# Side steps, softplus steps and sums: a new order on TensorE in a four-layer selective-scan kernel

## The chip, the cores and the metric

The kernel runs on one core of a Trainium2 chip. The metric is device time in microseconds (us) of one execution; the time of a kernel is the median of several executions.

## The reference, cut to what matters

Four layers are applied one after another to `x` of shape (8, 48, 48, 96): `x = x + layer(groupnorm(x))`. Each layer is a two-dimensional selective scan with 192 inner channels, 16 states per channel and four scan directions (rows, columns, and both backwards), over L = 2304 positions:

```python
xz = x @ in_proj_w.T;  xc, z = split(xz)            # 192 + 192 channels
u  = silu(depthwise_conv3x3(xc) + conv_b)
xs = 4 orders of u                                  # rows, columns, both reversed
dts, B, C = split(x_proj(xs))                       # rank r, 16 states, 16 states
delta = softplus(dt_proj(dts) + dt_bias)
h = exp(delta * A) * h + (delta * u) * B            # a scan over the 2304 positions
y = sum over the 16 states of h * C, plus u * D     # the four directions are added
out = (layernorm(y) * silu(z)) @ out_proj_w.T
```

Layers 0 to 2 are computed this way. Layer 3 writes the scan with cumulative sums and a division by the decay, and needs only the ends of the sequence when the decay fades; the kernel computes those ends and a test at the end decides whether the whole is needed.

## The kernel before, in words

Eight images are worked on in four pairs, so there are 3 x 4 = 12 (layer, pair) turns in the long part of the program. A turn has 12 groups (three tiles of 128 channels: image 0's first 128, image 1's first 128, and the last 64 of both; times two orders; times two directions). A group has three **chunks** of 768 positions, and a chunk has 16 **units**, n = 0 to 15, each for one 128 x 768 tile of states. That is 432 chunks and 6912 units. In this long part the instructions of each engine run in the order in which the program writes them (`keep_order`).

One unit k with its n is one pass of the loop in `run`. In the order of the text it issues:

- `collected()`: if a chunk's sum has been finished, ScalarE copies it out of PSUM (`collect`, line 887).
- `get_ready(k + 1)`: SyncE issues the loads of C (tile `cb`, nine buffers, four units ahead) and, for n in (2, 5, 7, 10, 13, 15), of B (tile `bb`, three buffers, five units ahead). For the other ten n, TensorE makes B of the next unit in PSUM (tile `b`, two buffers, line 678, `spread_rows`); for the six, GpSimd weighs `bb` with `du` (line 757, three units ahead) and ScalarE's exponential of the next unit goes to that PSUM buffer (line 780). So B(n) below is the product for unit n, issued in unit n - 1, and there is none for n in (2, 5, 7, 10, 13, 15).
- `c.scan(n)`: VectorE multiplies (line 810, only for the ten n with a B product) and scans (line 814); GpSimd multiplies `cb` by the result (line 823).
- The **sum** of unit k - 2: `add_up(n)` adds two `cb` tiles into the PSUM tile `acc` with `twin` (line 870, four recorded matmuls). It adds in pairs: `add_up` of an odd n is the first that needs `cb` of that n, from GpSimd; `add_up` of an even n brings nothing new and is the last use of both tiles of the pair before it, so it frees two `cb` buffers. Sum(16) is the second half of the pair (14, 15). `begin_sum` (line 855) starts a chunk's `acc` ahead of sum(1), and has to wait for the copy of the chunk before, since `acc` has one buffer.
- `beside()`: one step of `prepare` for the next chunk, and one side step. A side step is one step of the generators for the next turn's input (`prologue`: convolution, projections) or for the turn that is finished (`epilogue`: layer norm, gate, output product). They yield some 510 steps a turn.

`prepare` goes one step a unit, in two halves of 384 positions: the small product of `dts` (line 614) in units 15 and 6; ScalarE's functions (lines 622 to 628) in 0, 1 and in 7, 8; **softplus's sums** (line 634, two steps of eight recorded matmuls each, on tiles `du` and `dl`) in 2, 3 and in 9, 10; ScalarE's copies of `dl` (line 589) and VectorE's product with u in 4 and in 11, 12; the copies of `du` (line 589) in 5 and 13.

Before the change the sum comes ahead of `beside()` in a unit, with three exceptions. Sum(16) is issued two units after its chunk's sum(14), in unit 2 of the next chunk (`rest_of_sum`). In that unit (`ends`) no side step is taken. And in the unit after it, n = 3, where `collected()` had something to do (`busy`), `beside()` comes ahead of `begin_sum` and sum(1).

Of the kernel before, what the change touches and what calls it, by code (L numbers as in the profile page):

```python
# [53 lines left out]
NS = 16  # L54
# [49 lines left out]
def ss2d_layers_kernel(ctx: ExitStack, tc: tile.TileContext, x_in, consts, weights, out):  # L104
# [470 lines left out]
    def load_dt(c):  # L575
        r = layers[c.l].rank
        c.dts = sm1.tile([64, SCAN], F32, name="dts", tag="dts")
        for b in c.batches:
            q0 = 32 * b if c.t == 2 else 0
            nc.sync.dma_start(  # L580
                c.dts[q0 : q0 + r, : c.m],
                state[c.l, c.p]["xd"][c.ph, b, c.d * r : (c.d + 1) * r, c.c0 : c.c0 + c.m],
            )
# [101 lines left out]
    def store_some(n):  # L685
        for _ in range(min(n, len(late_stores))):
            o, z, at = late_stores.pop(0)
            nc.sync.dma_start(o[:, at], z[:, at])

    def collected():  # L690
        some = bool(late_sums)
        while late_sums:
            late_sums.pop(0)()
        return some

    def catch_up():
        while late_act:
            nc.scalar.copy(*late_act.pop(0))
# [450 lines left out]
    def drain(g):  # L1149
        for _ in g:  # L1150
            pass

    def step(g):
        next(g, None)
# [7 lines left out]
    def side_step(*sides):  # L1162

        for s in sorted(sides, key=lambda s: (not s.held, s.made / s.total)):
            got = next(s.g, s)
            s.held = got is True
            if got is not s and got is not GATED:
                s.made += 1
                return True
        return False  # L1170
# [3 lines left out]
    def mark():  # L1174
        marks.append(len(tc._region_blocks()[0].instructions))
# [12 lines left out]
    LAG = 2  # L1188
    LOADS, DECAYS = 3, 2

    def run(pairs, short):


        def units():
            for l, p in pairs:
                for gi, (t, ph, d) in enumerate(groups):
                    if l in short:
                        c = Edge(l, p, t, ph, d)
                        for i in range(NS // QUAD):
                            yield (l, p, gi * (NS // QUAD) + i), c, i  # L1200
                        continue
                    group = {}
                    for i in range(len(SCANS)):
                        c = Chunk(l, p, t, ph, d, i, group, c if d == 1 and i == 0 else None)
                        for n in range(NS):
                            yield (l, p, (gi * len(SCANS) + i) * NS + n), c, n

        def begin(l, p, first=False):
            if l not in layers:
                layers[l] = Layer(l)  # L1210
            return prologue(l, p, l in short, first)

        todo = list(units())

        def rest_of_sum(k):
            before = todo[k - 1][1] if k > 0 else None
            if isinstance(before, Chunk) and (k == len(todo) or todo[k][1] is not before):
                before.add_up(NS)

        def get_ready(k):  # L1220

            def early(ahead, what):
                for i in range(0 if k == 0 else k + ahead, min(k + ahead + 1, len(todo))):
                    getattr(todo[i][1], what)(todo[i][2])

            early(LOADS + 1, "load_b")
            early(LOADS, "load")
            if k == 0:
                todo[0][1].decay(todo[0][2])
            if k < len(todo):  # L1230
                (l, p, _), c, n = todo[k]
                if n == 0 and c.first and l not in short:
                    c.group["carry"] = capool.tile([P, NS], F32, name="carry", tag="carry")
                c.spread(n)
            early(DECAYS, "weigh")
            for i in range(k + DECAYS if k else 1, min(k + DECAYS + 1, len(todo))):
                todo[i][1].decay(todo[i][2])

        rest = begin(*pairs[0], first=True)
        while next(rest) is not READY:  # L1240
            pass
        rest = Side(rest)
        chunks = list(dict.fromkeys(c for _, c, _ in todo))
        drain(prepare(chunks[0]))
        behind = ahead = Side()
        coming = iter(())
        done = None
        mark()
        get_ready(0)
        for k, ((l, p, unit), c, n) in enumerate(todo):  # L1250
            at = pairs.index((l, p))
            following = pairs[at + 1] if at + 1 < len(pairs) else None
            if l in short and unit == 0:
                mark()
            per = NS // QUAD if l in short else NS
            all_units = len(groups) * (per if l in short else len(SCANS) * per)
            place["tiles"] = 3 * unit // all_units
            store_some(1)
            if done:
                behind, done = Side(epilogue(*done), 199), None  # L1260
            if unit == LAG and following:
                ahead = Side(begin(*following), 311)
            if k == 0:
                coming_to = 1
                coming = prepare(chunks[coming_to])
            if n == max(0, per - 1 - DECAYS):
                while coming_to < len(chunks) and not chunks[coming_to].ready:
                    next(coming)
            if n == 10 and coming_to + 1 < len(chunks):
                z = chunks[coming_to + 1]  # L1270
                if (z.l, z.p) == (l, p):
                    load_dt(z)
            busy = collected()
            get_ready(k + 1)
            catch_up()
            c.scan(n)
            if n == per - 1:
                drain(coming)
                if unit + 1 + per == all_units:
                    drain(behind.g)  # L1280
                    drain(ahead.g)
                coming_to = chunks.index(c) + 2
                coming = prepare(chunks[coming_to]) if coming_to < len(chunks) else iter(())


            def beside():
                step(coming)

                for _ in range(10 if l in short else 0 if ends else 1):
                    side_step(rest) or side_step(behind, ahead)  # L1290

            ends = l not in short and k > LAG and todo[k - LAG][2] == 0
            if busy and l not in short:
                beside()
            if k >= LAG:
                (bl, bp, _), b, bn = todo[k - LAG]
                rest_of_sum(k - LAG)
                if bl in short:
                    collected()
                b.add_up(bn)  # L1300
                if k > LAG and todo[k - LAG - 1][0][:2] != (bl, bp):
                    done = todo[k - LAG - 1][0][:2]
            if not (busy and l not in short):
                beside()
        for i in range(len(todo) - LAG, len(todo)):
            collected()
            rest_of_sum(i)
            todo[i][1].add_up(todo[i][2])
            catch_up()
        collected()  # L1310
        rest_of_sum(len(todo))
        collected()
        drain(epilogue(*pairs[-1]))

    last = NLAYER - 1
    run([(l, p) for l in range(NLAYER) for p in range(NPAIR)], (last,))

    keep_order(*marks[:2])
# [8 lines left out]
    with tc.If(nc.values_load(again, min_val=0, max_val=1) > 0):  # L1327
        run([(last, p) for p in range(NPAIR)], ())
# [95 lines left out]
```

## Time and profile before

| | |
|---|---|
| median of 5 runs | 20209.35 us (20192.55 to 20231.08) |
| profiled execution: own time / its span | 20228.16 us / 20226.3 us |
| busy over the span: PE, DVE, ACT, POOL | 83%, 87%, 80%, 88% |
| long part (layers 0 to 2), 178 to 18320 us | 18142 us: DVE busy 16758.65, POOL 17055.39, PE 15109.06, ACT 14719.72 us |
| layer 3 and the end, 18320 to 20226 us | 1906 us: PE busy 1569.34, ACT 1432.13 us |
| granted TensorE clock, long part | 0.91 |
| DMA share, long part | 0.86, 224 GB/s |

PE is TensorE, DVE VectorE, ACT ScalarE, POOL GpSimd, SP SyncE, which issues all loads. "Idle before" is the time for which an engine did nothing just before an instruction, and the name behind the arrow is what ended that time. In the long part a chunk takes 42.0 us (18142 / 432) and a unit 2.62 us.

### The profile page before, as it was taken

The numbers are of one execution on the slowest core, as the hardware profiler recorded it, in microseconds if no ns is written. First come the engines' busy times: TensorE is split into PE (matmuls) and PEld (weight loads), VectorE is DVE, ScalarE is ACT, GpSimd is POOL, SyncE is SP. The second block draws the span as 40 slices with busy tenths as digits, with TensorE's granted clock in tenths as the row PEclk, the third lists the DMA queues.
The fourth block names the chain that finished last, engine by engine and source line by source line (L and its number), as shares of the span: only waits on it lengthen the run. The fifth ranks groups of instructions, "written<-read, shape, count | busy, mean of one in ns | idle before, by whom it ended". The sixth has DMA issues, their size and how long they took to land.

```text
span 20226.3 us, 314848 instructions
## 1 busy us (share of the span) xinstructions
PE 16810.3 (83%) x92962; PEld 7791.0 (39%) x92962; DVE 17668.9 (87%) x14161; ACT 16225.3 (80%) x30014; POOL 17769.3 (88%) x10121
## 2 busy tenths in 40 slices
PE   7887887887888888888888888888888887888886
PEld 3333433333333333333333333333333333335555
DVE  6999998998999999999999999999999989996553
ACT  6777887887887887887887887877877877877786
POOL 6999999999999999999999999999999999995442
PEclk9998998998998999999998999998998988988997
DMA  5888888888888898888888888888888888884221
GB/s 157 229 226 223 227 224 217 226 223 218 224 228 224 223 232 223 225 228 224 223 229 222 222 226 224 222 224 220 223 224 222 224 221 222 219 219 115 80 74 50
DMA packets 2021150, 4200.80 MB, mean 208 GB/s; under 512 B 375920, under 2 KB 789360, under 8 KB 2017904
## 3 DMA queue, kind: packets, MB, share of 16 engines
q1 hardware_dynamic: 2019440, 4180.55, 79.5%
q8 instruction: 762, 12.48, 0.3%
q14 instruction: 948, 7.77, 0.2%
HBM read 4026.64 MB, written 152.27 MB: 207 GB/s over the span
## 4 chain that ended last, share of the span: by engine, by line
PE 21%; ACT 17%; DVE 14%; DMA 11%; issue 9%; POOL 3%; SPq 2%; DVEq 0%; POOLq 0%; ACTq 0%
DVE da L814 7%; PE acc L870 5%; PE ps L634 4%; DMA bb<-xd 4%; DMA cb<-xd 4%; DVE b L810 4%; ACT b L780 3%; ACT dl L589 3%; PE ps L314 3%; PE b L678 2%; ACT du L589 2%; POOL cb L823 2%; DVE bb L814 2%; ACT da L780 2%; SPq L740 1%
## 5 line engine op out<-in xcount | busy, mean ns | idle before, releaser
L823 POOL TENSOR_TENSOR cb<-cb,da 128x768 f32<-128x768 f32 x4320 | 7835.0, 1818 | 752.3 <-issue 258.2
L870 PE MATMUL acc<-cb,twin 128*64 128x384 f32 x27648 | 7206.5, 539 | 750.1 <-POOL cb L823 736.7
L814 DVE TENSOR_TENSOR_SCAN da<-da,carry,b 128x768 f32<-128x768 f32 x2880 | 5223.0, 1814 | 176.0 <-DVE b L810 1.4
L757 POOL TENSOR_TENSOR bb<-bb,du 128x768 f32<-128x768 f32 x2592 | 4717.1, 1820 | 236.5 <-DMA bb<-xd 131.1
L823 POOL TENSOR_TENSOR cb<-cb,bb 128x768 f32<-128x768 f32 x2592 | 4706.5, 1816 | 104.1 <-DVE bb L814 46.5
L810 DVE TENSOR_TENSOR b<-du,b 128x768 f32<-128x768 f32 x4320 | 4084.8, 946 | 707.3 <-PE b L678 603.7
L678 PE MATMUL b<-brow,pick 96*64 96x512 bf16 (+2 forms) x18816 | 2866.0, 354 | 1870.4 <-DVE da L814 1469.9
L780 ACT ACTIVATE da<-dl,a 128x768 f32<-128x768 f32 x4320 | 4011.6, 930 | 217.8 <-POOL cb L823 187.3
L870 PEld LDWEIGHTS acc<-cb,twin 128*64 128x64 f32 x27648 | 2450.1, 150 | 3042.8 <-POOL cb L823 1372.6
L814 DVE TENSOR_TENSOR_SCAN bb<-b,carry,bb 128x768 f32<-128x768 f32 x1728 | 3109.2, 1799 | 107.1 <-ACT b L780 37.0
L780 ACT ACTIVATE b<-dl,a 128x768 f32<-128x768 f32 x2592 | 2335.3, 901 | 608.5 <-DVE da L814 582.1
L678 PEld LDWEIGHTS <-pick 96*64 96x64 bf16 x18816 | 1084.1, 115 | 4140.0 <-DVE da L814 2681.6
L814 DVE TENSOR_TENSOR_SCAN da<-da,b 128x768 f32<-128x768 f32 x1440 | 2524.8, 1753 | 87.4 <-DVE b L810 0.5
L314 PE MATMUL ps<-pad,diag 128*64 128x480 f32 (+1 forms) x8640 | 2339.7, 568 | 32.9 <-ACT du L589 22.7
L589 ACT COPY dl<-ps 64x384 f32<-64x384 f32 x3456 | 1632.4, 472 | 708.7 <-PE ps L634 669.6
L634 PE MATMUL ps<-du,cst 128*64 128x384 f32 (+1 forms) x7296 | 1735.4, 512 | 75.4 <-ACT du L628 62.5
L589 ACT COPY du<-ps 64x384 f32<-64x384 f32 x3456 | 1633.4, 473 | 199.3 <-DVE ps L645 109.3
L814 DVE TENSOR_TENSOR_SCAN bb<-b,bb 128x768 f32<-128x768 f32 x864 | 1502.0, 1738 | 144.4 <-ACT b L780 76.5
L634 PE MATMUL ps<-dl,cst 128*64 128x384 f32 (+1 forms) x7296 | 1487.8, 483 | 0.0
L614 PE MATMUL ps<-dts,w 6*128 6x384 f32 (+5 forms) x2432 | 955.6, 602 | 205.8 <-DMA dts<-xd 106.6
L314 PEld LDWEIGHTS ps<-pad,diag 128*64 128x64 f32 x8640 | 753.3, 139 | 882.1 <-issue 727.6
L622 ACT ACTIVATE du<-ps,w 128x384 f32<-128x384 f32 (+1 forms) x912 | 519.9, 570 | 709.4 <-PE ps L614 694.6
(144 smaller groups left out, 19165.4 us busy)
## 6 DMA issues: line engine op xcount, KB each, us to landing
cb<-xd SPq DMA_DIRECT2D x13952, 192.0 KB
bb<-xd SPq DMA_DIRECT2D x5184, 192.0 KB
brow<-xb SPq DMA_DIRECT2D x864, 72.0 KB
ey<-yd SPq DMA_DIRECT2D x256, 216.0 KB
cb<-xd SPq DMA_DIRECT2D x128, 384.0 KB
yd<-y SPq DMA_DIRECT2D x216, 192.0 KB
ex<-xs SPq DMA_DIRECT2D x256, 108.0 KB
xb<-parts SPq DMA_DIRECT2D x96, 216.0 KB
```

What stands on the lines that cost most here:

```text
L314: nc.tensor.matmul(ps[half, :m], ly.diag[:, int(t == 2), j, half], pad[:, r0 + dy : r0 + dy + nr, dx : dx + W], start=(j == 0), stop=(j == 8),
L589: nc.scalar.copy(z[64 * h : 64 * h + 64, g, at], v[64 * g : 64 * g + 64])
L614: nc.tensor.matmul(o[:, :m], ly.dtw[q0 : q0 + r, k, chans], dts[q0 : q0 + r, at], start=True, stop=True,)
L622: nc.scalar.activation(e, v, AF.Abs, bias=bias)
L634: nc.tensor.matmul(v[half], ident[:, half], z1, start=(i == 0), stop=(i == 3))
L678: nc.tensor.matmul(o[64 * h : 64 * h + 64], pick[:, b, n : n + 1].to_broadcast([2 * NR, 64]), rows, start=True, stop=True,)
L757: nc.gpsimd.tensor_mul(b, b, self.du[n % 2])
L780: nc.scalar.activation(da, self.dl[n % 2], AF.Exp, scale=layers[self.l].a2[:, int(self.t == 2), n % 2, k, i : i + 1],)
L810: nc.vector.tensor_mul(b, self.du[n % 2], b)
L814: nc.vector.tensor_tensor_scan(way(h), way(da), way(b), start, ALU.mult, ALU.add)
L823: nc.gpsimd.tensor_mul(c, c, h)
L870: nc.tensor.matmul(self.acc[64 * g : 64 * g + 64, a, : self.m // 2], twin, c[:, a, :], start=False, stop=(pair + 2 == NS and not self.turns),)
```

## The change

Three things move; nothing is added to or taken from the arithmetic.

- In every unit the step of `prepare` and the side step are issued between B and the sum, where the sum came first.
- Sum(16) is issued together with sum(15), in unit 1 of the next chunk and not in unit 2; so `collected()` copies `acc` out in unit 2 and not in unit 3.
- Side steps by unit: none in n = 3, 9 and 10 (`full`); in n = 12 and 14 (`free`, where there is no B product to issue) a second one behind the sum; one in every other n, 2 included. Before it was none in n = 2 and one in every other. Both make 15 a chunk.

In layer 3 the step of `prepare` is issued ahead of the sum, and the ten side steps stay behind it; that part is put in order by the scheduler, not by `keep_order`.

```diff
+    full, free = (3, 9, 10), (12, 14)
+
     def run(pairs, short):
...
-        def rest_of_sum(k):
-            before = todo[k - 1][1] if k > 0 else None
-            if isinstance(before, Chunk) and (k == len(todo) or todo[k][1] is not before):
-                before.add_up(NS)
+        def sum_of(c, n):
+            c.add_up(n)
+            if isinstance(c, Chunk) and n == NS - 1:
+                c.add_up(NS)
...
-            busy = collected()
+            collected()
             get_ready(k + 1)
             catch_up()
             c.scan(n)
...
-            def beside():
-                step(coming)
-
-                for _ in range(10 if l in short else 0 if ends else 1):
+            def beside(some):
+                for _ in range(some):
                     side_step(rest) or side_step(behind, ahead)
 
-            ends = l not in short and k > LAG and todo[k - LAG][2] == 0
-            if busy and l not in short:
-                beside()
+            step(coming)
+            if l not in short:
+                beside(n not in full)
             if k >= LAG:
                 (bl, bp, _), b, bn = todo[k - LAG]
-                rest_of_sum(k - LAG)
                 if bl in short:
                     collected()
-                b.add_up(bn)
+                sum_of(b, bn)
                 if k > LAG and todo[k - LAG - 1][0][:2] != (bl, bp):
                     done = todo[k - LAG - 1][0][:2]
-            if not (busy and l not in short):
-                beside()
+            beside(10 if l in short else n in free)
         for i in range(len(todo) - LAG, len(todo)):
             collected()
-            rest_of_sum(i)
-            todo[i][1].add_up(todo[i][2])
+            sum_of(todo[i][1], todo[i][2])
             catch_up()
-        collected()
-        rest_of_sum(len(todo))
         collected()
         drain(epilogue(*pairs[-1]))
```

## The prediction

> **What bounds the kernel now.** I read the page's busy times first, then the waits, then the order of time on PE, and last SyncE's own waits. The stretches' busy times split the span:
>
> ```profile
> 178.00:18320.00 18142.00, 15109.06 (x81627) 6637.35 (x81629) 16758.65 (x12601) 14719.72 (x27223) 17055.39 (x9680) 0.91 0.86 224
> 18320.00:20226.00 1906.00, 1569.34 (x10806) 1101.85 (x10802) 899.75 (x1538) 1432.13 (x2664) 708.04 (x424) 0.89 0.26 71
> ```
>
> The columns are PE, PE's weight loads, DVE, ACT, POOL, then clock, DMA share and GB/s. In the long part POOL is busy for 94% and DVE for 92%, so POOL can win at most 18142 - 17055 = 1087 us and DVE 1383. A chunk costs POOL 22 products of 1.82 us, 40.0 us of its 42.0. No engine alone is the bound; time is lost where one hands over late. The waits name the places:
>
> ```profile
> PEld acc L870 <- POOL cb L823: 1372.6, 1045, 4.8
> ACT dl L589 <- PE ps L634: 669.6, 414, 4.8
> DVE b L810 <- PE b L678: 603.7, 646, 10.5
> POOL cb L823 <- issue: 272.8, 311, 7.7
> DVE b L810 <- PE acc L870: 93.5, 67, 4.8
> ```
>
> (us in total, times, longest.) DVE loses 603.7 + 93.5 = 697 us to a B that comes late. I gave each idle stretch to the unit whose scan ends next (6912 scans, 16 a chunk). Of the 697 us, 260 lie at n = 1, 196 at n = 11, 55 at n = 12, 67 at n = 6, 44 at n = 3, 38 at n = 0. POOL's 1088 us: 249 at n = 2, 163 at n = 7, 139 at n = 15, 110 at n = 0, 83 at n = 10, 59 at n = 12. PE in order of time shows how n = 11 and 12 come about:
>
> ```profile
> 9002.08 0.19 PEld L870 LDWEIGHTS acc<-cb,twin 128*64 128x64 f32 x2 [2.46 <-POOL cb L823]
> 9002.53 1.70 PE L634 MATMUL ps<-du,cst 128*64 128x384 f32 x7
> 9004.16 1.05 PE L472 MATMUL ps<-u,w 128*96 128x480 f32 x2
> 9005.14 0.52 PE L678 MATMUL b<-brow,pick 96*64 96x512 bf16 x4
> 9005.70 0.96 DVE L810 TENSOR_TENSOR b<-du,b 128x768 f32<-128x768 f32 x1 [0.51 <-PE b L678]
> 9006.14 1.46 PE L634 MATMUL ps<-dl,cst 128*64 128x384 f32 x8
> 9007.64 1.94 ACT L589 COPY dl<-ps 64x384 f32<-64x384 f32 x4 [1.55 <-PE ps L634]
> ```
>
> In unit 9 PE stands 2.46 us at sum(7) until GpSimd has made cb(7); only then come softplus's first sums, a side step (a projection) and B(11), for which DVE waits. None of what stood behind the sum needed cb(7). Over 432 chunks sum(7) starts 1.96 us before cb(7) is done and lasts 3.02 us where 0.81 is usual.
>
> **The change part by part.**
>
> *Softplus's sums ahead of sum(7) (units 9, 10).* Eight matmuls take 1.3 us start to start (9002.53, less the overlap, to 9004.16 with the eighth in front). They fit into the wait of 1.96. Side step 9, 0.67 us of PE in the mean (0 to 1.25), leaves, and side step 10, 0.64, too. Between cb(7) and B(11) stand only the tail of sum(7), 1.06 us, in place of 1.06 + 1.3 + 0.67 = 3.03. B(11) starts 1.08 us after its buffer is free (scan 9), so it can come 1.08 sooner and no more; its end is late by up to 1.5 us in nine of ten chunks (against scan 10), and the idle mean is 196 / 432 = 0.45. B(12) starts 2.05 us after its buffer is free and gains more. I take 200 of the 196 + 55 = 251 us off DVE, and most of ACT's 669.6 us wait for the same sums. DVE's time counts only where POOL then waits less: POOL's idle in n = 10 to 15 is 83 + 37 + 59 + 9 + 21 + 139 = 348 us, part of it for loads. Bounds: 60 (POOL already lags by a product at n = 10 and 11 and hides it) and 300. A measure from the trace: in 88 chunks where units 9 and 10 happen to have no side work on PE, scans 8 to 15 take 20.50 us, against 20.80 in the rest; 0.30 x 432 = 130 us for that half of the edit alone. I take 150 us of gain.
>
> *All other odd sums behind the steps.* Sums 5, 11 and 13 wait less (they last 1.11, 0.94, 1.15 us against 0.81); with sum(13) in a late B(1) at most 0.3 us a chunk. What is behind them on PE is the same B as before. I take 30 us, bounds 0 and 110.
>
> *Sum(16) a unit sooner, side step 3 to unit 2.* B(3) now stands behind sum(16): 0.74 us at full clock, 1.3 at half. PE waits 327 us in 320 chunks for scan 1 before B(3), 0.76 us a chunk, and B(3)'s end is a median 1.07 ahead of need; sum(15) lasts 1.85 us, so side step 1 slips into its wait. Cover is there in most; where PE is cold it is missing. Cost 25 us, bounds 0 and 120. B(4) trades sum(16) for side step 2, B(6) loses and gains one step: nothing. The copy of `acc` on ACT goes from unit 3 to unit 2; it waits for PE for 264 us now and would for sum(16) again, but ACT's own queue there holds a carry and, two units on, an exponential: nothing. Buffers of cb(14), cb(15) come free a unit sooner, before load cb(7).
>
> *Second side steps in 12 and 14.* They take 2 x 0.66 us of PE where PE waits for DVE's buffers, 464 us at n = 13 and 607 at n = 15 (3.0 us a chunk with the smaller waits). Hidden as long as that lasts. But B(12) now comes about 1.5 us sooner, so PE's wait there is about 3.0 + 1.5 - 1.3 - 0.6 (DVE sooner) = 2.6 us: little less than before.
>
> That matters for the clock. The chunk's start runs on PE at half rate:
>
> ```profile
> 9018.29 0.85 PE L678 MATMUL b<-brow,pick 96*64 96x512 bf16 x4 [3.43 <-DMA brow<-xb]
> 9020.35 1.54 PE L614 MATMUL ps<-dts,w 16*64 16x384 f32 x4
> 9024.56 0.96 DVE L810 TENSOR_TENSOR b<-du,b 128x768 f32<-128x768 f32 x1 [2.58 <-PE b L678]
> ```
>
> B took 0.85 us here and 0.52 above; the granted clock was 0.57 from 9016 to 9032 and 1.00 from 9000 to 9009. In all chunks, half rate holds 1.89 of the 2.89 us of unit 0 and 1.88 of the 3.42 of unit 1, and 7.7 us of a chunk. From the waits I take no gain at n = 1 beyond the 30 us above: 2.6 against 3.0 us. The Trainium skill ("TensorE: Matmul & The Clock Gate", section "Part 1: The HAM clock gate (the "warmup" mystery)") says that the clock is halved only after an idle window of about 3.4 us, and is whole again after as long a busy one; by that rule a step in the middle of the wait of units 14 and 15 would keep the clock up in most chunks, and the sum would be some 150 us lower. The trace goes cold in most chunks with waits that mean 1.4 to 1.9 us each, which speaks against so sharp a rule, so it is a rival and not in the sum.
>
> *Sums that free buffers for loads come later.* SyncE issues in order:
>
> ```profile
> SPq L740 <- PE acc L870: 1859.4, 1736, 6.5
> POOL bb L757 <- DMA bb<-xd: 131.1, 108, 4.4
> ```
>
> Most of the 1859 us belong to cb(5) on sum(14) (620 us, 293 times), cb(9) on sum(2) (303), cb(15) on sum(8) (293), cb(13) on sum(6) (198). Queued behind cb(15) on SP: both `brow` loads, cb(0) and bb(2). bb(2) lands a median 1.08 us before POOL takes it, within 0.2 in a quarter of the chunks; POOL idles 140 us there. The others land 2.4 to 3.6 us ahead. Sum(8) ends 4.21 us after cb(7) now; after the change, scan 9 (1.95 after cb(7)) + B 0.52 + softplus 1.3 + sum 0.81 = 4.6, later by 0.4. In the tight quarter to half that is 45 to 85 us; sum(14) and sum(6) behind one side step more (0.7 us) eat margin that is there. I take 50, bounds -40 (DVE sooner moves scan 9 too) and 150. The dts wait (95 us at n = 1, at a new turn) now holds sum(13) too: 11 x 0.7 = 8 us, dropped. Layer 3: order of ten steps and a sum, 0 +- 15.
>
> **Sum**, against the profiled execution (20228.2): -150 - 30 + 25 + 0 + 50 = -105; I add -35 (bounds 0 and -100) for ACT, which starts the copies of `dl` sooner (634 of its 669.6 us fall at n = 11) and so makes the exponentials of 13 and 15 in time more often; DVE and POOL idle for that kind of wait some 113 and 23 us. That gives -140, 20088. The median of the runs lies 18.8 lower: **20070**.
>
> **Rivals.**
>
> *Loads turn late (slower).* Place: SP behind cb(15), in unit 10; price: bb(2) later by 0.65 to 1.3 us (half or all of the softplus step) in half of the chunks, 140 to 280 us of POOL's idle. POOL's 139 us at n = 15 then stay too, so of the first part's 150 some 60 are kept, with the 30 of the odd sums 90: 20209 + 50 to + 190, that is 20260 to 20400. It decides once sum(8) is later than bb(2)'s 1.08 us. For: the quarter already at 0.2. Against: three units until POOL needs it move with POOL itself.
>
> *POOL hides it all (no change).* DVE's stalls shrink, POOL only lags more: 20209 less 0 to 40. For: POOL's 94%, and it idles just 37 us at n = 11. Against: 139 us at n = 15, where it waits for scan 14.
>
> *The clock stays up (much faster).* Units 0 and 1 at full rate: B took 0.85 there and 0.52 at full rate, so what stands between B(0) and B(1) shrinks by some 40%, and of B(1)'s 260 us only the 95 of the dts wait and a few more stay: 150 less, 20070 - 150 = 19920; with the upper bound of the first part (300 for 150), 19770.
>
> **How the numbers follow.** A measurement of this kernel can tell 0.2%, 40 us, from no change. Main case 0.46 (19960 to 20165); clock rival 0.16 (19770 to 19960); no change 0.14; slower 0.24 (20250 to 20400, the loads above all). Faster 0.62, same 0.14, slower 0.24. The likeliest case's own range is 19960 to 20165. Low end 19800 leaves out some 0.05, high end 20310 some 0.1.
>
> **What would show it.** Right: `ACT dl <- PE ps L634` far below 669.6; DVE's wait for B at n = 11 and 12 below 50 us in place of 251; fewer of PE's waits for `cb`. Clock: granted share in the long part above 0.91 says the rival is there. Wrong: POOL's wait for `bb` above 200 us and SP's for `acc` above 2000; DVE's wait at n = 3 far over 44; DVE's stalls gone and POOL's lag at n = 15 grown, with the span unchanged.

## The result and the profile after

The change moves the time by nothing that can be measured: a median of 20209.06 us (20169.15 to 20232.01, 24 runs) against 20209.79 us before (20179.68 to 20263.55, 44 runs), ratio 0.9996, 95% interval 0.999 to 1.0001. The forecast of 20070 us was wrong.

The profiled execution of after took 20186.67 us, with a span of 20184.9 us. It lies 22 us below its kernel's median, and that of before 18 us above, so the 41 us between the two profiles are not a difference of the kernels.

The same rows as before, first the stretches (PE, weight loads, DVE, ACT, POOL, clock, DMA share, GB/s):

```profile
178.00:18280.00 18102.00, 15035.59 (x81602) 6564.60 (x81602) 16730.54 (x12593) 14754.05 (x27209) 17035.83 (x9675) 0.91 0.87 224
18280.00:20185.00 1905.00, 1557.16 (x10828) 1091.53 (x10828) 906.84 (x1542) 1437.05 (x2675) 715.20 (x428) 0.89 0.26 72
```

In the long part POOL is busy for 94% and DVE for 92%, as they were, and the clock is 0.91 still. Layer 3 takes what it took. The waits (us in total, times, longest):

```profile
PEld acc L870 <- POOL cb L823: 1120.6, 1176, 5.2
...
DVE b L810 <- PE b L678: 660.3, 523, 12.7
...
PEld ps L614 <- ACT du L589: 418.6, 308, 5.9
...
POOL bb L757 <- DMA bb<-xd: 184.6, 161, 4.8
ACT dl L589 <- PE ps L634: 178.3, 181, 4.2
...
POOL cb L823 <- issue: 163.5, 154, 9.0
```

ACT's wait for softplus's sums fell from 669.6 to 178.3 us: that part did what was forecast. But DVE's wait for B is 663 us in all (3 of them put down to `acc`) where it was 603.7 + 93.5 = 697. By unit (each idle stretch given to the unit whose scan ends next, as in the prediction) it fell from 196 to 31 us at n = 11, from 55 to 4 at n = 12 and from 67 to 18 at n = 6; it rose from 38 to 102 at n = 0, 44 to 113 at n = 3, 10 to 66 at n = 8, 260 to 280 at n = 1. The stalls have moved. Two rows above are new in size: PE's wait in the product of `dts` (L614) for ScalarE's copies of `du`, and POOL's wait for `bb`, which was 131.1. The first was, before:

```profile
PEld ps L614 <- ACT du L589: 221.2, 209, 4.6
```

POOL has the same work in both kernels, so its idle time shows where time was won and lost. Given to the instruction in front of which it lies (long part, 432 chunks), it fell before the product of cb(14) from 130 to 65 us and before that of cb(6) from 161 to 87; it rose before the weighing of bb(2) from 132 to 209, of bb(5) from 41 to 76 and of bb(7) from 13 to 46, and before the product of cb(8) from 31 to 58. Told by VectorE's scans, units 8 to 15 of a chunk take 20.39 us where they took 20.74, 151 us less over all chunks, and units 0 to 7 take 21.53 us where they took 21.24, 125 us more. So there is a gain, and it is paid back half a chunk later.

PE in order of time, unit 9 and on:

```profile
8422.17 1.51 PE L634 MATMUL ps<-du,cst 128*64 128x384 f32 x8
...
8423.46 0.86 PE L870 MATMUL acc<-cb,twin 128*64 128x384 f32 x4
...
8425.91 0.51 PE L678 MATMUL b<-brow,pick 96*64 96x512 bf16 x4 [1.59 <-DVE da L814]
...
8426.26 1.46 PE L634 MATMUL ps<-dl,cst 128*64 128x384 f32 x8
...
8427.48 0.94 DVE L810 TENSOR_TENSOR b<-du,b 128x768 f32<-128x768 f32 x1
...
8427.55 0.81 PE L870 MATMUL acc<-cb,twin 128*64 128x384 f32 x4
...
8427.77 1.94 ACT L589 COPY dl<-ps 64x384 f32<-64x384 f32 x4
...
8428.20 0.49 PE L678 MATMUL b<-brow,pick 96*64 96x512 bf16 x4
...
8429.52 1.54 SPq L765 DMA_DIRECT2D brow<-xb  x2
```

Softplus's first sums now run ahead of sum(7) (8423.46). B(11) at 8425.91 waits for nothing but its buffer, which scan 9 sets free; DVE's product at 8427.48 and the copies of `dl` at 8427.77 wait for nothing. Then the second softplus step stands ahead of sum(8), which starts at 8427.55. SyncE's own waits:

```profile
SPq L740 <- PE b L678: 1366.5, 1133, 7.8
SPq L740 <- PE acc L870: 1353.5, 1129, 9.2
```

The second row was, before:

```profile
SPq L740 <- PE b L678: 460.6, 750, 6.8
```

The prediction looked for an `acc` row above 2000 us. That row alone fell from 1859.4 to 1353.5 and would acquit the loads. But a load that a sum sets free can be put down to another instruction on PE near it, B here: the two rows together went from 2320 to 2720 us. By load, the wait before cb(11), which takes the buffer that sum(4) frees, went from 139 to 829 us, and that before cb(15), on sum(8), from 310 to 426. Unit 6 in order of time, in the same chunk of both kernels, shows the first. Before:

```profile
8403.50 3.64 SPq L740 DMA_DIRECT2D cb<-xd  x6
...
8404.12 1.51 PE L870 MATMUL acc<-cb,twin 128*64 128x384 f32 x8
...
8406.56 0.91 PE L614 MATMUL ps<-dts,w 16*128 16x384 f32 x2 [0.93 <-ACT du L589]
...
8408.72 0.51 PE L678 MATMUL b<-brow,pick 96*64 96x512 bf16 x4
...
8410.10 0.94 DVE L810 TENSOR_TENSOR b<-du,b 128x768 f32<-128x768 f32 x1
```

After:

```profile
8412.54 8.21 SPq L740 DMA_DIRECT2D cb<-xd  x6
...
8413.27 1.93 ACT L589 COPY du<-ps 64x384 f32<-64x384 f32 x4
...
8415.25 0.91 PE L614 MATMUL ps<-dts,w 16*128 16x384 f32 x2 [1.71 <-ACT du L589]
...
8418.09 1.55 PE L870 MATMUL acc<-cb,twin 128*64 128x384 f32 x4
...
8419.43 0.80 PE L678 MATMUL b<-brow,pick 96*64 96x512 bf16 x4
...
8420.27 0.96 DVE L810 TENSOR_TENSOR b<-du,b 128x768 f32<-128x768 f32 x1 [1.40 <-PE b L678]
...
8420.86 1.18 SPq L740 DMA_DIRECT2D bb<-xd  x2
```

The product of `dts` needs the PSUM bank that ScalarE copies `du` out of until 8415.20. Before the change sum(4) stood ahead of it (the second half of the eight at 8404.12) and used this time. Now sum(4) stands behind it and behind the unit's side step (on PE from 8416.23 to 8418.16), and starts at 8418.09. B(8) comes behind the sum, DVE waits 1.40 us for it, and SyncE takes 8.21 us over six loads that stand in a row, where it took 3.64. In the mean over all chunks sum(4) starts 1.26 us after scan 6 does; before, it started 0.97 us ahead of it.

### The profile page after: what moved, and what is told of

Same layout as the page of the kernel before. It is cut to its first block, busy times and chain, and to the rows that moved or that the text cites. A ratio compares the mean times of both kernels' runs of the same rounds, so it can differ in the third digit from the quotient of the medians.

```text
span 20184.9 us, 315179 instructions
## 1 busy us (share of the span) xinstructions
PE 16716.2 (83%) x92962; PEld 7703.6 (38%) x92962; DVE 17653.8 (87%) x14161; ACT 16266.4 (81%) x30014; POOL 17760.0 (88%) x10121
## 4 chain that ended last, share of the span: by engine, by line
PE 17%; ACT 17%; DVE 15%; DMA 14%; issue 9%; SPq 3%; POOL 2%; DVEq 0%; ACTq 0%; POOLq 0%
DVE da L814 7%; DMA cb<-xd 6%; DMA bb<-xd 5%; DVE b L810 4%; PE acc L870 4%; ACT b L780 3%; PE ps L634 2%; ACT dl L589 2%; ACT du L589 2%; PE ps L314 2%; ACT da L780 2%; PE b L678 2%; SPq L740 2%; DVE bb L814 2%; DMA brow<-xb 2%
## 5 line engine op out<-in xcount | busy, mean ns | idle before, releaser
L870 PE MATMUL acc<-cb,twin 128*64 128x384 f32 x27648 | 7056.9, 539 | 449.2 <-POOL cb L823 427.0
L814 DVE TENSOR_TENSOR_SCAN da<-da,carry,b 128x768 f32<-128x768 f32 x2880 | 5223.0, 1814 | 177.2 <-ACT carry L698 1.9
L757 POOL TENSOR_TENSOR bb<-bb,du 128x768 f32<-128x768 f32 x2592 | 4716.9, 1820 | 373.1 <-DMA bb<-xd 184.6
L780 ACT ACTIVATE da<-dl,a 128x768 f32<-128x768 f32 x4320 | 4016.4, 931 | 449.8 <-POOL cb L823 417.6
L870 PEld LDWEIGHTS acc<-cb,twin 128*64 128x64 f32 x27648 | 2361.3, 148 | 3553.9 <-issue 2168.7
L780 ACT ACTIVATE b<-dl,a 128x768 f32<-128x768 f32 x2592 | 2337.6, 902 | 1097.9 <-DVE da L814 997.6
L814 DVE TENSOR_TENSOR_SCAN bb<-b,carry,bb 128x768 f32<-128x768 f32 x1728 | 3110.0, 1800 | 91.6 <-ACT b L780 59.2
L814 DVE TENSOR_TENSOR_SCAN da<-da,b 128x768 f32<-128x768 f32 x1440 | 2524.8, 1753 | 87.3 <-DVE b L810 1.4
L678 PEld LDWEIGHTS <-pick 96*64 96x64 bf16 x18816 | 1156.1, 116 | 3766.1 <-DVE da L814 2244.1
L314 PE MATMUL ps<-pad,diag 128*64 128x480 f32 (+1 forms) x8640 | 2172.4, 563 | 69.5 <-DVE eyc L1086 32.0
L589 ACT COPY du<-ps 64x384 f32<-64x384 f32 x3456 | 1632.9, 472 | 234.5 <-DVE ps L645 115.9
L589 ACT COPY dl<-ps 64x384 f32<-64x384 f32 x3456 | 1631.6, 472 | 219.3 <-PE ps L634 178.3
L634 PE MATMUL ps<-du,cst 128*64 128x384 f32 (+1 forms) x7296 | 1585.1, 503 | 254.2 <-ACT du L628 239.2
L814 DVE TENSOR_TENSOR_SCAN bb<-b,bb 128x768 f32<-128x768 f32 x864 | 1501.8, 1738 | 155.0 <-ACT b L780 112.4
L614 PE MATMUL ps<-dts,w 6*128 6x384 f32 (+5 forms) x2432 | 916.0, 574 | 392.0 <-ACT du L589 213.9
L314 PEld LDWEIGHTS ps<-pad,diag 128*64 128x64 f32 x8640 | 665.1, 138 | 771.6 <-issue 571.8
L634 PEld LDWEIGHTS ps<-du,cst 128*64 128x64 f32 x7296 | 626.1, 143 | 859.8 <-ACT du L628 441.0
```

Of the source, the lines that this page charges most:

```text
L314: nc.tensor.matmul(ps[half, :m], ly.diag[:, int(t == 2), j, half], pad[:, r0 + dy : r0 + dy + nr, dx : dx + W], start=(j == 0), stop=(j == 8),
L589: nc.scalar.copy(z[64 * h : 64 * h + 64, g, at], v[64 * g : 64 * g + 64])
L614: nc.tensor.matmul(o[:, :m], ly.dtw[q0 : q0 + r, k, chans], dts[q0 : q0 + r, at], start=True, stop=True,)
L634: nc.tensor.matmul(v[half], ident[:, half], z1, start=(i == 0), stop=(i == 3))
L678: nc.tensor.matmul(o[64 * h : 64 * h + 64], pick[:, b, n : n + 1].to_broadcast([2 * NR, 64]), rows, start=True, stop=True,)
L757: nc.gpsimd.tensor_mul(b, b, self.du[n % 2])
```

## The experiments

All edits are on the kernel before unless after is named; orders and side steps are changed in layers 0 to 2 only. Each time is a median with its ratio to the runs of before on the same chip; each ratio is turned into us with 20209. The expectations take the plain difference of the medians instead, so that the first gain below is 69 us there and 59 here. Each kernel also has a profile; what is said of single waits comes from that one execution.

**The parts alone.** Steps ahead of the sum in units 9 and 10 only:

```diff
-            if busy and l not in short:
+            early = l not in short and (busy or n in (9, 10))
+            if early:
                 beside()
...
-            if not (busy and l not in short):
+            if not early:
                 beside()
```

> The kernel before, with one part of the change: in units 9 and 10 alone the softplus step and the side step are issued ahead of the sum. Theory A (the change's gain at n = 11 and 12 is real and its other parts give it back): VectorE's wait for B at n = 11 and 12 falls from 251 us to under 100, and the time by 60 to 130 us. Theory B (POOL and the loads are the bound and hide it): the wait falls as much, the time stays within 40 us of the kernel before and POOL's lag behind the scans grows.

20131.64 us, 0.9971 (0.9959 to 0.9982): 59 us gained. The forecast had 150 for this with the side steps gone from the two units. The wait for B at n = 11 and 12 fell as expected, to 97 us. ACT's wait for the sums is 182.2 us, as far down as in after, but DVE still waits 645.6 us for B, and POOL 183.9 us for `bb`.

The side steps' places only:

```diff
-                for _ in range(10 if l in short else 0 if ends else 1):
+                some = (n not in (3, 9, 10)) + (n in (12, 14))
+                for _ in range(10 if l in short else some):
```

> The kernel before, with the change's count of side steps by unit alone (none in 3, 9, 10; two in 12 and 14; one in 2), all in the old place. Theory A: B(11) and B(12) lose 0.67 and 0.64 us of PE ahead of them, the wait for B there falls by about half, the time by 30 to 90 us. Theory B: within 40 us of the kernel before.

20089.14 us, 0.9944 (0.993 to 0.9957): 113 us gained with every sum where it was, more than either theory had. First its waits, then its long part:

```profile
DVE b L810 <- PE b L678: 386.1, 325, 9.4
...
DVE b L810 <- PE acc L870: 100.9, 64, 4.6
...
POOL bb L757 <- DMA bb<-xd: 97.8, 80, 3.8
```

```profile
178.00:18100.00 17922.00, 14979.77 (x81332) 6692.44 (x81332) 16643.97 (x12536) 14681.44 (x27121) 16972.24 (x9630) 0.93 0.85 225
```

DVE's wait for B is 210 us less: at n = 11 and 12 it fell from 251 to 129 us, since no side step stands there any more, and at n = 1 from 260 to 191. The clock is 0.93; PE runs at half rate for 6.37 us of a chunk, where it was 7.74. How much of the 113 us comes by the clock and how much by the free places at n = 11 and 12, no run separates.

Sum(16) a unit sooner only (side steps and order as before; the steps of unit 3 stay ahead of its sum):

```diff
-        def rest_of_sum(k):
...
+        def sum_of(c, n):
+            c.add_up(n)
+            if isinstance(c, Chunk) and n == NS - 1:
+                c.add_up(NS)
...
-            busy = collected()
+            collected()
+            busy = n == 3
...
-                rest_of_sum(k - LAG)
...
-                b.add_up(bn)
+                sum_of(b, bn)
```

> The kernel before, with sum(16) in unit 1 and the copy of acc in unit 2, all else as before (the steps of unit 3 stay ahead of begin_sum). Theory A: B(3) stands behind one sum more, VectorE's wait for it grows from 44 us to 80 to 120, the time by 20 to 70 us. Theory B: within 40 us of the kernel before.

20230.88 us, 1.0017 (1.0007 to 1.0026): 34 us lost, where 25 were forecast for this and a side step. DVE's wait at n = 3 is 105 us for 44, and POOL's idle time before bb(7) 44 us for 13.

The order only, in every unit:

```diff
-            if busy and l not in short:
+            if l not in short:
                 beside()
...
-            if not (busy and l not in short):
+            if l in short:
                 beside()
```

> The kernel before, with the steps ahead of the sum in every unit; side steps by unit and sum(16) as before. Theory A: the gain at n = 11 of the first of these kernels, given back at n = 8 (the dts product of unit 6 ahead of sum(4)) and at the loads: SP's waits on PE grow, POOL's wait for bb(2) from 140 to 200 us, the time within 40 us of the kernel before. Theory B: the same time, but then the first of these kernels shows no gain either.

20309.27 us, 1.0054 (1.0041 to 1.0068): 109 us slower, where both theories had at most 40. Units 9 and 10 together gain 59, so other units lose more.

**Which units.** From here on the form of the first diff with other units:

```diff
+            early = l not in short and (busy or n in (9,))                    # unit 9 only
+            early = l not in short and (busy or n in (6,))                    # unit 6 only
+            early = l not in short and (busy or n in (0, 2, 4, 8, 12, 14))    # the other even ones
```

> The kernel before, with the steps ahead of the sum in unit 9 alone (the first run did it in 9 and 10 and won 69 us). Theory L (a step ahead of a sum that frees cb buffers makes the loads behind it late): without the step ahead of sum(8) in unit 10, SP's wait for PE before cb(15), 310 us before and 809 in the first run, goes back to about 300, B(0) and bb(2) are as before, and the gain is larger than the 69 us: 90 to 160. Theory P (only the place on PE counts): softplus's second sums in unit 10 come later than in the first run, the gain is smaller: 30 to 69 us.

Unit 9 only: 20094.28 us, 0.9945 (0.9931 to 0.9958), 111 us gained. Unit 10, in the first experiment, took away half of that.

The same with the side steps' places of the change (second diff):

> The kernel before, with the change's side steps by unit and the steps ahead of the sum in unit 9 alone. Theory L: the two gains add in part (112 from the side steps, some 50 more from unit 9, where B(11) still waited 127 us in the run with side steps alone): 140 to 200 us below the kernel before, POOL idle under 900 us in the long part. Theory P: no more than the side steps alone, 90 to 130 us.

20051.01 us, 0.9928 (0.9915 to 0.9942): 146 us gained, against 113 and 111 for its halves. Both save the same stalls of DVE at n = 11 and 12 (39 us left), so they overlap; the clock's share is kept (6.3 us of a chunk at half rate). Its rows:

```profile
DVE b L810 <- PE b L678: 462.7, 410, 11.9
...
POOL bb L757 <- DMA bb<-xd: 98.3, 102, 3.6
```

> The kernel before, with the steps ahead of the sum in unit 6 alone: there the product of dts waits for a PSUM bank that ScalarE's copies of du still hold, and sum(4) now stands behind it. Theory L: SP's wait for PE before cb(11) grows from 136 us to 600 or more, VectorE's wait for B(8) from 10 to 60 us, the time by 40 to 110 us. Theory P: PE's other units decide; the time within 30 us of the kernel before.

Unit 6 only: 20289.85 us, 1.0043 (1.0029 to 1.0057), 87 us lost. The rows of the changed kernel's unit 6 are there by themselves:

```profile
PEld ps L614 <- ACT du L589: 347.2, 263, 5.0
```

SyncE waits 947 us before cb(11), and DVE 52 us at n = 8 where it waited 10. POOL's idle time before bb(2), a load that stands in the queue behind cb(11), went from 132 to 198 us, and before the product of cb(8) from 31 to 56. This is the unit that the prediction did not look at.

> The kernel before, with the steps ahead of the sum in units 0, 4, 8, 12 and 14 and, in unit 2, the softplus step ahead of sum(16). All these sums free cb buffers and none waits for POOL. Theory L: every load waiting on them is later by a side step, 0.7 us: cb(5), cb(9), cb(13); POOL's wait for bb(7) and bb(10) grows, the time by 20 to 90 us. Theory P: nothing that PE makes for VectorE moves; the time within 30 us of the kernel before.

The other even units: 20406.42 us, 1.0101 (1.0085 to 1.0116), 204 us lost, more than twice what either theory had.

**Undoing, and a tenth buffer.** In the changed kernel, the sum first again in units 6 and 10:

```diff
-            step(coming)
-            if l not in short:
-                beside(n not in full)
+            late = l not in short and n in (6, 10)
+            if not late:
+                step(coming)
+                if l not in short:
+                    beside(n not in full)
...
-            beside(10 if l in short else n in free)
+            if late:
+                step(coming)
+                beside(n not in full)
+            else:
+                beside(10 if l in short else n in free)
```

> The changed kernel with the sum ahead of the steps again in units 6 and 10, where a run before cost 87 us (unit 6) and 39 us (unit 10, the difference of two runs). Theory A (the parts add up): 100 to 140 us faster than the kernel before, SP's waits for PE before cb(11) and cb(15) back under 150 and 350 us. Theory B (something else in the change gives the gain back): within 50 us of the kernel before.

20094.17 us, 0.9949 (0.9935 to 0.9962). The two units cost the changed kernel 0.47%, 95 us, and POOL's idle time before bb(2) says where: 118 us here, 209 in the changed kernel. Its rows for the `dts` product and `bb` are back near those of before:

```profile
DVE b L810 <- PE b L678: 537.1, 440, 12.4
...
PEld ps L614 <- ACT du L589: 272.8, 245, 5.2
...
POOL bb L757 <- DMA bb<-xd: 137.0, 107, 4.8
```

SyncE waits 115 us before cb(11) again and 173 before cb(15).

All odd units with the side steps' places (second diff, and `n in (1, 5, 7, 9, 11, 13, 15)`):

> The kernel before with the change's side steps by unit and the steps ahead of the sum in every odd unit; in even units the sum first, sum(16) in unit 2. Theory A: the odd units but 9 add little, since their sums wait little: 140 to 190 us faster than the kernel before (the run with 9 alone was 151). Theory P (steps ahead of sum(13) and sum(11) put work in front of B(0) and B(1)): 30 to 100 us slower than that run.

20079.39 us, 0.9938 (0.9924 to 0.9951). With unit 9 alone it was 0.9928: the intervals overlap, so the other odd sums bring nothing that can be measured, where 30 us were forecast. The time lies between the two theories.

Ten `cb` buffers, in after and in before (the mean matrix is loaded into a working tile to make the room):

```diff
-    cbpool = ctx.enter_context(tc.tile_pool(name="cb", bufs=9))
+    cbpool = ctx.enter_context(tc.tile_pool(name="cb", bufs=10))
...
-    cst = cpool.tile([P, 2 * P + DM], F32, name="cst")
+    cst = cpool.tile([P, P + DM], F32, name="cst")
...
+    mean_w = tmp.tile([P, P], F32, name="mean", tag="tmp")
```

> The changed kernel with a tenth cb buffer (the mean matrix is loaded into a passing tile to make room), so that a load of cb waits for a sum a unit older. Theory L (unit 6 and 10 cost through loads that wait for sum(4) and sum(8)): SP's waits for PE before cb(11) and cb(15) shrink to a third, and the change shows its gain: 80 to 160 us faster than the kernel before with ten buffers. Theory P (they cost through B(8) and B(11) on PE): no more than 40 us faster than that.

> The kernel before with the same tenth cb buffer, as the base for the run above. Theory L: bb(2) and brow come sooner, POOL's 140 us wait for bb(2) shrinks, 20 to 80 us faster than with nine. Theory P: within 30 us.

After: 20080.29 us, 0.9936 (0.9923 to 0.995). Before: 20140.01 us, 0.9965 (0.9952 to 0.9979). The buffer is worth 0.6% in the changed kernel and 0.35% in the old one (the difference of 0.25% has an uncertainty of 0.2). So loads held up by late sums cost both kernels time, the changed one more. With ten buffers the changed kernel is 60 us ahead of the old one, between the two theories: its waits before cb(11) and cb(15) are 42 and 47 us and POOL's idle time before bb(2) is 65 us, but DVE's wait at n = 8 is still 74 us. In after with ten, POOL's wait is a third (the code lies two lines lower):

```profile
POOL bb L759 <- DMA bb<-xd: 64.3, 64, 3.3
```

**What was still open:** how unit 6's cost splits, where the other even units lose, and unit 10 by itself.

> The kernel before with a tenth cb buffer and the steps ahead of the sum in unit 6 alone; its base is the kernel before with ten buffers (20140, 0.9965 of the kernel before), and with nine buffers unit 6 cost 87 us. Theory L (the cost is the loads behind cb(11)): 0 to 30 us over its base, that is 20140 to 20170. Theory P (the cost is B(8) on PE, behind the dts product and sum(4)): 50 to 90 us over it, 20190 to 20230, with VectorE's wait for B(8) near 50 us as with nine buffers.

Unit 6 with ten buffers: 20188.08 us, 0.9986 (0.9977 to 0.9995), which is 0.21% or 42 us above before with ten, between the two theories; 87 us were lost with nine. The 45 us between the two costs have an uncertainty of some 43, so the times alone hardly show that the loads matter. The profiles split the cost: with nine buffers unit 6 raised POOL's idle time before bb(2) by 66 us and before the product of cb(8) by 25; with ten it is 80 us before bb(2), for 77 in its base, and 59 before the product of cb(8), for 33. So with nine the larger part went by the loads, and with ten B(8) is what is left. SyncE waits some 50 us before cb(11) here (68 in the base), and DVE 60 at n = 8. No run took B(8) away alone.

> The kernel before with a tenth cb buffer, the change's side steps by unit and the steps ahead of the sum in unit 9 alone. With nine buffers that was 0.9928 of the kernel before; the tenth gave 0.9965 to the kernel before and less is left of POOL's wait for bb(2) (93 us). If the gains add: 20000 (0.990). If POOL's work is now the bound: 20030 to 20060, no better than with nine.

Side steps, unit 9 and ten buffers: 20015.83 us, 0.9895 (0.988 to 0.9911), the fastest version of this study, some 210 us ahead of both kernels; 0.9928 x 0.9965 is 0.9893, so the two gains add.

Unit 2 only, and unit 10 only (`n in (2,)`, `n in (10,)`):

> The kernel before with the softplus step ahead of sum(16) in unit 2 alone (no side step is taken there). Theory Y (the copy of acc, first in ScalarE's queue in unit 3, waits for sum(16), behind it the copies of dl, and VectorE's product with u waits for those): DVE idle before unit 5's scan from 294 ns a chunk to about 800, the time by 150 to 230 us, most of the 204 us that the even units cost together. Rival (the cost of the even units is spread, by loads): 0 to 60 us.

20332.92 us, 1.0062 (1.0049 to 1.0076): 125 us lost, below the 150 to 230 expected for all that the even units lose, and far above the rival's 60. Here softplus's first sums stand ahead of sum(16), and ScalarE, whose queue in unit 3 begins with the copy of `acc`, waits for it and takes the copies of `dl` late. Its rows, then those of before:

```profile
ACT y L887 <- PE acc L870: 715.5, 344, 7.1
...
DVE ps L642 <- ACT dl L589: 240.8, 164, 75.6
...
DVE ps L645 <- ACT dl L589: 183.4, 192, 5.3
```

```profile
ACT y L887 <- PE acc L870: 264.0, 254, 4.7
...
DVE ps L642 <- ACT dl L589: 130.1, 99, 81.6
...
DVE ps L645 <- ACT dl L589: 66.5, 100, 4.1
```

DVE's idle time before scan 5 went from 107 to 339 us, and POOL's before the products of cb(5) and cb(6) from 35 to 95 and from 161 to 204. The rival has a sign too: SyncE's wait before cb(7), on sum(16), went from 126 to 633 us. But POOL's idle time before the product of cb(7) is 12 us for 11, and before bb(2) 128 for 132, so those late loads do not show on POOL. In after, sum(16) is out a unit before, and the first row is 202.1 us. The remaining 80 us of the other even units' 204 were not taken apart.

> The kernel before with the steps ahead of the sum in unit 10 alone. Theory L: SP's wait for PE before cb(15) from 310 to 700 us or more, bb(2) and brow later, the time by 20 to 60 us (9 and 10 together won 39 us less than 9 alone). Theory P: softplus's second sums come 0.8 us sooner, ScalarE waits less for them, the time 10 to 40 us shorter.

20271.68 us, 1.0027 (1.0018 to 1.0036): 55 us lost, near the top of what the theory of late loads gave. Its rows, for 131.1, 1859.4 and 460.6 us before:

```profile
POOL bb L757 <- DMA bb<-xd: 212.1, 194, 4.2
```

```profile
SPq L740 <- PE acc L870: 1571.3, 1449, 6.5
SPq L740 <- PE b L678: 897.0, 760, 7.1
```

SyncE waits 1007 us before cb(15) in place of 310. Behind it stand `brow`, cb(0) and bb(2), and bb(2), which landed a mean of some 1.2 us before POOL took it, lands some 0.5 us before; POOL's idle time before it is 227 us for 132. DVE's wait at n = 11 grew too, from 196 to 242 us. No run has unit 10 alone with ten buffers, so that the loads carry the cost is read from the trace.

## Why the prediction was wrong

The account in us, as a chain of kernels: side steps and unit 9 gain 146 (0.9928). Sum(16) a unit sooner and the new order in all other units but 6 and 10 take 43 of it away (0.9949; sum(16) alone costs 34). Units 6 and 10 take 95 more (0.9996), and 8 are left. Each link has an uncertainty of some 30 to 40 us. The costs of single units on the kernel before do not simply add up to this: 87 and 55 for units 6 and 10, and 204 for the other even ones, 125 of it in unit 2, where the changed kernel has no sum. The forecast had 215 of gains and 75 of costs: 69 too much of the one, and 63 too little of the other.

*The step that failed: "Sums that free buffers for loads come later", 50 us, where units 6 and 10 cost 95.* Its place was right: POOL's idle time before bb(2) went from 132 to 209 us. Its shift of sum(8) was near: that sum ends 4.44 us after cb(7) in place of 4.21, where 4.6 was forecast. (Unit 10 alone costs 55, but there sum(8) ends 6.13 us after cb(7).) What was left out is unit 6. The prediction put the step as "sum(14) and sum(6) behind one side step more (0.7 us) eat margin that is there": it counted PE's work in the moved step, and not the wait that the step brings along. In unit 6 the moved step holds a product that needs a PSUM bank back from ScalarE. For the same product in unit 15 a wait was weighed, for its load at a new turn ("11 x 0.7 = 8 us, dropped"); for unit 6, with sum(4) behind it, none was, though the table of waits before had `PEld ps L614 <- ACT du L589` at 221.2 us. So sum(4) came 2.2 us later, where 0.7 was counted for the sums that were named. A sum that stood ahead of this wait was free; behind it, it held up cb(11), the loads after cb(11) as far as bb(2), and B(8). How the 95 us divide between units 6 and 10 in the changed kernel, no run shows.

*Softplus's sums ahead of sum(7): 150, with 35 for ACT.* The step held two edits, the order and the side steps that leave units 9 and 10. The mechanism was right: 31 + 4 us are left at n = 11 and 12, where less than 50 was forecast, and ACT's row fell as forecast. The two halves are worth 111 (in unit 9) and 113 us alone and 146 together, so the 150 was near; units 8 to 15 of the changed kernel take 151 us less. The comparison of chunks with and without side work (130) came close to its half. The step gave unit 10 as a place of the gain, where the order costs. And the 35 for ACT did not come: the wait that it was to shorten, VectorE's for ScalarE's exponentials (`DVE bb L814 <- ACT b L780`), went from 113.5 to 171.7 us, and the kernel with side steps and unit 9, where ACT's row is still 493.9 us, is faster than the one with units 9 and 10, where it is 182.2. One reading of the shown rows was too large: the 2.46 us at sum(7) are the idle time of the weight loads, and PE itself stood 1.79.

*All other odd sums, 30:* nothing measurable. *Sum(16), 25:* 34 us; its place, n = 3, shows 113 us for 44, one of the signs named for being wrong.

*Second side steps in 12 and 14, 0, no gain at n = 1:* half right. DVE's stall at n = 1 is 280 us in the changed kernel, but 191 with the side steps' places alone. The rival that the clock stays up is seen there too, at a small size: half rate takes 6.37 us of a chunk in place of 7.74, and 7.36 in the changed kernel. Its sign, a granted clock above 0.91 in the long part, came with the side steps' places alone (0.93) and not in the changed kernel (0.91).

*The rivals.* "POOL hides it all" gave the right number for a wrong reason: four kernels with shorter stalls of DVE (0.9944, 0.9945, 0.9928, 0.9949) are all faster, so POOL does not hide them. POOL's work is the same in all, so its idle time in the long part goes with the time: 1088 us before, 1066 after, 953 with the side steps, 921 with unit 9 too, 1185 with the order alone. "Loads turn late" had the right kind of cost and one of its two places, but a price that did not fit: the gain and the loss came out equal. Its signs in the profile missed it: POOL's wait for `bb` is 184.6 us and not above 200, and SyncE's `acc` row 1353.5 us and not above 2000, because part of that wait changed its name.

## What to carry to other kernels

Before a step is moved ahead of another on one queue, list what each of its instructions waits for, not only what it costs: sum(4) came 2.2 us later behind a step whose own work is 0.9 us and a side step. Then ask who takes over what the delayed one sets free. The odd sums here set nothing free and could stand behind other work at no cost that can be measured; the even ones were dear behind a wait (unit 6) and behind plain work too (unit 10), since loads stand in a queue for what they set free. An edit of several parts that comes out at zero should be taken apart: here the two parts that pay were worth 0.72% without the rest.

## What the runs showed of the hardware

TensorE's time at half clock went from 7.74 to 6.37 us of a chunk when three of 15 small side steps were moved out of units 3, 9 and 10 into 2, 12 and 14, with the same work in all. The Trainium skill ("TensorE: Matmul & The Clock Gate", section "Part 1: The HAM clock gate (the "warmup" mystery)") puts the change of clock at an idle window of about 3.4 us in a free-running grid. The trace of before agrees with a grid: 1145 of its 1146 stretches of one clock are multiples of 3.41 us long. It does not agree with an idle window alone. In the long part the clock was halved 518 times, in 319 of the 432 chunks, and PE had 71 idle stretches of more than 3.4 us; its waits for DVE at n = 13 and 15 mean 1.4 and 1.9 us. In the 3.41 us ahead of a fall PE was busy for 0.39 of the time in the median (nine in ten lie between 0.09 and 0.65). Stretches of 3.41 us after which the full clock stayed had 0.40 at the least and 0.98 in the median. So in this trace a window that is busy for less than about half can halve the clock.

A buffer that was set free late cost more further back in the queue than at its own load. SyncE's wait before cb(11) went from 139 to 829 us, and POOL's idle time before the product of cb(11) from 57 to 45; before the weighing of bb(2), some loads behind cb(11), it went from 132 to 209.
